# Two edge sorts of a graph kernel: records turned to column order by ScalarE, places summed on TensorE, loads and features reordered

## The chip, the cores and the metric

The kernel runs on one core of one Trainium2 chip. The metric is the device time of one execution in microseconds (us). The core has five engines with instruction streams of their own: TensorE (PE, matrix products, with weight loads, PEld, beside them), VectorE (DVE), ScalarE (ACT), GpSimd (POOL) and SyncE (SP, which here only issues transfers). Transfers (DMA) can be issued by SP, ACT and POOL, each a queue of its own.

## The reference

It has four residual stages on x of 3,125 nodes by 256 features. Source, destination, edge type and edge weight of 53,125 edges are given.

```
x = x + L0_gnn(layernorm(x), (src, dst), edge_weight)      # 4 heads of 64
x = x + L0_ffn(layernorm(x))                               # 16 experts, top 2
x = x + L1_gnn(layernorm(x), rel_emb, src, dst, edge_type) # 200 relations
x = x + L1_ffn(layernorm(x))                               # top half of the tokens

# L0_gnn
feats = einsum('nd,hdo->hno', x, Ws) + bs[:, None, :]
a_s = einsum('hno,ho->hn', feats, aw[:, :O]); a_d = einsum('hno,ho->hn', feats, aw[:, O:2*O])
score = a_s[:, src] + a_d[:, dst] + aw[:, 2*O][:, None] * elem[None, :] + ab[:, None]
w = exp(-relu(score / 20.0))
out = segment_sum(w * feats[:, dst], src) / segment_sum(w, src)
# L0_ffn: per expert, hidden = silu(x @ w1) * (x @ w2); out = hidden @ w3, weighted
# L1_gnn: agg = segment_sum((h[src] + rel_emb[etype]) @ weight_neighbor * alpha, dst)
#         alpha = exp(leaky_relu(score))[:, None], divided by its sum over that axis of one
#         out = relu(agg) + h @ (loop weights)
```

Both graph stages sum over the edges of each node. So the kernel needs the edges grouped by node: sort s0 by `src` for the first graph stage, sort s1 by `dst` for the second.

## The kernel before, in words

The nodes form NT = 25 blocks of 128. The edges lie in a table of 128 partitions by EC = 416 columns, seen as NS = 13 slices of SC = 32 columns; a group is SJ = 8 columns. An edge becomes a record of V fields of f16: 5 in s0 (other node, place in its block, three pieces of the weight's bits), 3 in s1. `sort_edges` makes the generator `ranking` (`load_in`, then `places`), 13 steps `move` and a function `load`.

`load_in` loads segment, other end and value (`load_edges`) and cuts them into digits `dig`. `bf` holds each edge's block number.

`places` computes where each edge goes. First it counts: for each block a one-hot comparison over the 416 columns (`hot`, L377, on DVE and POOL in turn in s0), then on PE for each of the 32 columns of a slice a matmul with all-ones weights and one with strictly-before weights over the 25 x 13 = 325 values of that column (L383; they stand 32 elements apart). From the counts come the start of each block and slice (`base`, L422). Then a loop over 25 blocks (L431 to L445) makes `x`, 1 where the edge is of block b, adds `base` to the first column of each slice, makes a running sum (`cum`, L437), keeps it where the edge is of block b (`own`, L441), and adds that into `pos` (L444, on POOL in s0). 13 rounds of three operations `ge` (L487, L493, L498) find the target rows `to` of the records' chunks; from `pos` come `pp` and `kp`, partition and place in a chunk.

`move(s)` handles a slice of 32 columns, in 4 groups of 8. A group makes on DVE the one-hots `hp` (L545, 128 x 8) and `hk` (L550, 40 x 8) and their product with the digits, `hv` (L555, NK x V x 8 elements: 1,600 in s0, 960 in s1; the 8 columns lie innermost). Then 8 matmuls per group (L560), with `hp[:, :, j]` as weights and `hv[:, :, :, j]` moving, accumulate in PSUM. After 4 groups ACT copies the sum out (`rec`, L566) and 5 indirect transfers on POOL scatter the chunks into the DRAM table `tab` (L569). `load` reads the table (`tk`, L588, on SP), turns it on PE (L601), and makes index, row and value of 440 edge tiles.

The order is that of the instruction streams that a scheduler makes from the program order; each engine then runs its own stream in order. `run` builds constants, zeroes the two edge tables (`edge_table`, SP transfers from a zero tile), makes the sort's constants, runs the s0 ranking, loads x, moves s0, zeroes the sums `sums0` and `sums1` of the two graph stages (`zero_sums`, L298: a POOL memset and SP transfers each), and then calls `heads_features` (weights `w_feat` and bias `b_feat` loaded on SP, extended by the products with `aw` at L858 and L861; for each of 25 blocks of normalised x two transposes L173, two matmuls L873, a bias addition on DVE L877; the table `table0` written by SP) and `load`. `heads_edges` gathers feature rows by indirect transfers (L754) and sums edges on PE (L798), with the s1 ranking as fill between its groups. `experts` runs 65 expert tiles (token rows gathered L1119, turned L173, products L1130 and L1147, Silu L1135) and calls one s1 `move` step in each of the first 13 tiles. Relation stage and token stage follow.

## Time and profile before

| what | value |
| --- | --- |
| runs | 2841.39, 2849.33 (median), 2865.01 us |
| the profiled execution | 2845.15 us, span 2842.8 us, mean granted clock 0.822 |
| PE busy | 1878.6 us, 66% |
| DVE busy | 1446.3 us, 51% |
| POOL busy | 1167.4 us, 41% |
| ACT busy | 390.7 us, 14% |
| first matmul of the s0 moves | at 170.1 us |
| first edge gather of the heads' stage | at 429.71 us |
| gathers of edge rows, L754 | 880, 848.6 us busy on POOL |
| s1 and s0 moves on PE, L560 | 832, 246.8 us busy |

Times inside the span count from the first instruction. The engine's busy time says how long it worked, not whether anything waited for it. A line such as `L560 PE MATMUL s_mv<-s_hv,s_hp 128*128 128x200 f16 x416 | 150.5, 543 | 89.9 <-DVE s_hv L555 89.9` names source line, engine, operation, output and inputs, shape and number of instructions; then the busy time in us and the mean of one in ns (overlapping matmuls make that mean longer than their distance); then the engine's idle time before them and what ended it. PEclk is the granted clock of PE as a share of full speed.

### The profile page before, as it was taken

What the parts mean: (1) busy time and instruction counts of PE and PEld (TensorE: products, weight loads), DVE (VectorE), ACT (ScalarE), POOL (GpSimd) and SP (SyncE); (2) the same over time, 40 slices, a digit from 0 to 9 for tenths busy, and PEclk for the clock granted to TensorE, in tenths of its full rate; (3) what the DMA queues carried; (4) which work ended last, traced back from release to release, by engine and by line L of the source; (5) the groups of instructions that cost most, each with busy time, mean ns of one, the idle gap of its engine ahead of it and who ended that gap; (6) DMA issues with size and microseconds to landing.
All of it is one profiled execution on the core that took longest, in us unless ns stands there. A gap on an engine that the chain in (4) does not pass through costs nothing.

```text
span 2842.8 us, 24381 instructions
## 1 busy us (share of the span) xinstructions
PE 1878.6 (66%) x7534; PEld 1126.4 (40%) x7534; DVE 1446.3 (51%) x3397; ACT 390.7 (14%) x1097; POOL 1167.4 (41%) x1198
## 2 busy tenths in 40 slices
PE   3169554854544443399999991447878778785298
PEld 0024232543433332356666660323434334343166
DVE  4876225476665343644422224445655556549721
ACT  0000010010000000100112120112222222221012
POOL 4235306576654646034411115036666666650000
PEclk9999996676666667577799996768889888898599
DMA  2000325343444433144499982254545455431000
GB/s 83 0 3 5 104 89 137 93 130 112 115 100 114 116 100 101 49 150 130 131 316 318 317 291 84 87 156 131 148 129 148 130 142 149 128 85 34 8 21 18
DMA packets 258938, 334.04 MB, mean 118 GB/s; under 512 B 30861, under 2 KB 192407, under 8 KB 258807
## 3 DMA queue, kind: packets, MB, share of 16 engines
q1 hardware_dynamic: 197527, 191.26, 21.3%
q0 software_dynamic: 51920, 132.68, 17.6%
q10 hardware_dynamic: 9360, 8.52, 0.9%
q8 instruction: 61, 1.00, 0.1%
q14 instruction: 70, 0.57, 0.1%
HBM read 298.38 MB, written 33.98 MB: 117 GB/s over the span
## 4 chain that ended last, share of the span: by engine, by line
PE 39%; DVE 14%; issue 10%; POOL 9%; another core or an unknown queue 8%; DMA 4%; ACT 1%; SPq 0%; DVEq 0%; POOLq 0%; ACTq 0%
PE ps_sums L798 10%; PE ps_h L1130 9%; POOL rows L754 9%; PE ps_y L1147 4%; PE s_mv L560 3%; DVE cmp L1426 3%; PE ps_hid L1453 3%; PE ps_out L1464 3%; DMA rows<-table,s_idx 3%; DVE msg L926 2%; DVE hot L771 2%; PE ps_x_t L173 1%; PE ps_h_t L173 1%; PE ps_f L1264 1%
## 5 line engine op out<-in xcount | busy, mean ns | idle before, releaser
L754 POOL DMA_INDIRECT rows<-table,s_idx x880 | 848.6, 964 | 725.0 <-issue 240.4
L798 PE MATMUL ps_sums<-msg,oh 128*128 128x260 f32 x880 | 306.6, 519 | 261.8 <-DVE msg L926 143.1
L798 PE MATMUL ps_sums<-rows,ohw 128*128 128x457 f32 x880 | 414.0, 616 | 62.8 <-ACT ohw L1319 54.1
L798 PEld LDWEIGHTS ps_sums<-msg,oh 128*128 128x128 f32 x880 | 226.6, 265 | 325.1 <-issue 250.1
L560 PE MATMUL s_mv<-s_hv,s_hp 128*128 128x200 f16 (+1 forms) x832 | 246.8, 472 | 89.9 <-DVE s_hv L555 89.9
L798 PEld LDWEIGHTS ps_sums<-rows,ohw 128*128 128x128 f32 x880 | 179.0, 215 | 217.5 <-issue 149.6
L1130 PE MATMUL ps_h<-w,x_t 128*128 128x512 f32 x520 | 256.1, 638 | 0.0
L771 DVE TENSOR_SCALAR hot<-wide,pcols 128x768 bf16<-128x768 bf16 (+1 forms) x296 | 175.4, 597 | 73.9 <-PE ps_near L780 63.0
L560 PEld LDWEIGHTS <-s_hp 128*128 128x128 f16 x832 | 122.1, 147 | 208.7 <-issue 180.3
L762 DVE TENSOR_TENSOR oh<-ps_hold,s_row 128x768 f32<-128x768 f32 (+1 forms) x148 | 139.9, 946 | 125.7 <-remote 73.5
L1119 POOL DMA_INDIRECT xg<-xtab,who x65 | 61.9, 952 | 345.1 <-PE ps_x_t L173 302.6
L569 POOL DMA_INDIRECT s_tab<-s_rec,s_to x130 | 147.8, 1137 | 115.1 <-ACT s_rec L566 78.9
L780 PEld LDWEIGHTS <-hot 128*128 128x128 bf16 x1760 | 70.0, 98 | 212.3 <-issue 149.2
L1136 DVE TENSOR_TENSOR hid<-hid,ps_h 128x512 f32<-128x512 f32 x65 | 44.7, 688 | 210.3 <-ACT hid L1135 204.4
L1319 ACT ACTIVATE ohw<-oh,s 128x128 f32<-128x128 f32 x440 | 136.5, 388 | 106.6 <-DVE s L1282 75.2
L1130 PEld LDWEIGHTS ps_h<-w,x_t 128*128 128x128 f32 x520 | 102.8, 209 | 105.7 <-issue 105.5
L926 DVE TENSOR_TENSOR msg<-rows,ps_hold 128x1536 f32<-128x1536 f32 x74 | 128.1, 1731 | 2.0 <-ACT ps_hold L924 1.9
L787 DVE TENSOR_REDUCE near<-ps_near 128x24 f32<-128x72 f32 (+2 forms) x148 | 29.4, 198 | 190.3 <-remote 150.2
L1147 PE MATMUL ps_y<-w,h_t 128*128 128x256 f32 x520 | 122.9, 379 | 0.7 <-ACT h_t L175 0.7
L1147 PEld LDWEIGHTS ps_y<-w,h_t 128*128 128x128 f32 x520 | 98.7, 190 | 41.7 <-issue 30.6
L545 DVE TENSOR_TENSOR s_hp<-num_p,s_pp 128x1024 f16<-128x1024 f16 x104 | 71.8, 690 | 82.8 <-PE s_mv L560 81.4
L1313 DVE TENSOR_TENSOR rows<-ps_hold,s_val 128x1200 f32<-128x1200 f32 x74 | 101.1, 1367 | 6.1 <-PE ps_sums L798 6.1
(307 smaller groups left out, 2344.2 us busy)
## 6 DMA issues: line engine op xcount, KB each, us to landing
w<-in_L_ffn_w_dram SPq DMA_DIRECT2D x195, 512.0 KB
wide<-s_w SPq DMA_DIRECT2D x72, 576.0 KB
rows<-table,s_idx POOLq DMA_INDIRECT x880
ytab<-y ACTq DMA_DIRECT2D x65, 128.0 KB
sums<-sums_z SPq DMA_DIRECT2D x5, 1142.5 KB
more<-sums SPq DMA_DIRECT2D x25, 228.5 KB
sums<-sums_z SPq DMA_DIRECT2D x5, 650.0 KB
table<-f SPq DMA_DIRECT2D x5, 650.0 KB
```

The lines of the kernel that those rows point to most:

```text
L560: nc.tensor.matmul(ps[:, : NK * V], hp[:, :, j], rec[:, :, :, j].rearrange("p k v -> p (k v)"), start=(j0 + j == 0), stop=(j0 + j == C - 1),)
L569: d = nc.gpsimd.indirect_dma_start(out=tab, out_offset=bass.IndirectOffsetOnAxis(ap=to[:, i : i + 1], axis=0), in_=out[:, k * CH * V : (k ...
L754: nc.gpsimd.indirect_dma_start(out=rows[:, j, :width], out_offset=None, in_=table, in_offset=bass.IndirectOffsetOnAxis(ap=st["idx"][:, k + ...
L762: nc.vector.tensor_tensor(oh[:, :n, :], numbers[:, None, :P].to_broadcast(sh), st["row"][:, k : k + n, None].to_broadcast(sh), op=OP.is_equal,
L771: nc.vector.tensor_scalar(t[:, : n // 2, :], w, at, None, op0=OP.is_equal)
L798: nc.tensor.matmul(ps[:, :W], oh[:, j, :], msg[:, j, :], start=(head and j == 0), stop=(last and j == n - 1),)
L926: nc.vector.tensor_tensor(msg[:, :n, :HO].rearrange("p j (h o) -> p j h o", o=O), rows[:, :n, :HO].rearrange("p j (h o) -> p j h o", o=O), ...
L1130: nc.tensor.matmul(ph[:, i * HID : (i + 1) * HID], xt[:, c, :], w12[:, i, c, :], start=(c == 0), stop=(c == C - 1),)
L1147: nc.tensor.matmul(py[:, :D], ht[:, c, :], w3[:, c, :], start=(c == 0), stop=(c == HC - 1))
L1313: nc.vector.tensor_tensor(rows[:, :n, R0:], self.numbers[:, None, :R].to_broadcast(sh), st["val"][:, k : k + n, None].to_broadcast(sh), op ...
L1319: nc.scalar.activation(ow[:, j, :], oh[:, j, :], AF.Copy, scale=s[:, 1, j : j + 1])
L1426: nc.vector.tensor_scalar(cmp[:, s:e], wrow[:, s:e], w, None, op0=op, op1=OP.add, accum_out=rank[:, t, i : i + 1],)
```

## The change

The change has six parts.

1. Loads: `load_edges` fills only the partitions from 96 on with padding, on DVE. The s0 edges are loaded first, then x; the zeroing of the edge tables moves out of `edge_table` into `zero_table`, called after the loads (s0) and after the features' weights (s1).
2. Counts of s0 (`roomy`): block numbers as bf16 with columns outermost (`bt`), compared with a table of block numbers (`num_b`) in 4 DVE operations of 2,600 elements; `hot` has columns outermost, so that the 64 matmuls read 325 elements in one piece.
3. Places of s0: ACT copies `x` from `hot`; PE sums `pos` in PSUM by 26 matmuls with the identity; the operations `ge` take up to 7 slices at once.
4. Moves of both sorts: ACT copies the group's records `hv` (in `rec`) into `col`, where the records of one column lie in one piece, and the matmuls read `col`. The s1 moves are cut into halves: 26 steps in 26 expert tiles.
5. `load` of s0 issues its reads from POOL's queue.
6. `heads_features` is split: `heads_weights` before the moves, the features after moves and `load`. The bias is added by a third matmul (`top`, a matrix whose first row is ones, times `bias`), ACT copies the result out, and ACT's queue writes `table0`. The sums are zeroed last in program order.

```diff
@@ -224,7 +224,7 @@
-        engine.memset(dst, pad)
+        engine.memset(dst[96:, :], pad)
         done = 0
@@ -286,6 +286,11 @@
+        return tab
+    def zero_table(self, name, tab):
+        nc, CH, n = self.nc, self.CH, self.MT + self.OT
+        V = tab.shape[1] // CH
         with self.tc.tile_pool(name=f"{name}_init", bufs=1) as pool:
@@ -293,7 +298,6 @@
-        return tab
@@ -329,15 +333,15 @@
-            return rp.tile([P, EC], dt, tag="row", name=f"{name}_{nm}", bufs=16 if roomy else 7)
+            return rp.tile([P, EC], dt, tag="row", name=f"{name}_{nm}", bufs=8 if roomy else 7)
...
-            self.load_edges(seg_i, seg, self.NP, help)
+            self.load_edges(seg_i, seg, self.NP, nc.vector)
             oth_i = tmp(I32, "oth")
-            self.load_edges(oth_i, other, 0, help)
+            self.load_edges(oth_i, other, 0, nc.vector)
             val = tmp(F32 if bits else I32, "val")
-            self.load_edges(val, value, 0, help)
+            self.load_edges(val, value, 0, nc.vector)
             yield
@@ -345,6 +349,9 @@
+            if roomy:
+                st["bt"] = tl([P, C, NS], BF16, "bt")
+                nc.vector.tensor_copy(st["bt"], bi.rearrange("p (s t) -> p t s", t=C))
@@ -368,8 +375,27 @@
-            piece = NT if roomy else -(-NT // 2)
-            for b0 in range(0, NT, piece):
+            if roomy:
+                num_b = tl([P, n], BF16, "num_b").rearrange("p (b s) -> p b s", s=NS)
+                nc.vector.tensor_copy(
+                    num_b, self.iota[:, :NT, None].to_broadcast([P, NT, NS])
+                )
+                hot = tl([P, C, n], BF16, "hot")
+                for t0 in range(0, C, J):
+                    sh = [P, J, NT, NS]
+                    nc.vector.tensor_tensor(
+                        hot[:, t0 : t0 + J, :].rearrange("p t (b s) -> p t b s", s=NS),
+                        num_b[:, None].to_broadcast(sh),
+                        st["bt"][:, t0 : t0 + J, None, :].to_broadcast(sh), op=OP.is_equal,
+                    )
+                    for w, ps in ((self.ones_h, tot), (self.before_h, pre)):
+                        for t in range(t0, t0 + J):
+                            nc.tensor.matmul(
+                                ps[:, :n], w, hot[:, t, :], start=(t == 0), stop=(t == C - 1)
+                            )
+            piece = -(-NT // 2)
+            for b0 in () if roomy else range(0, NT, piece):
                 m = min(piece, NT - b0)
@@ -426,23 +452,37 @@
-            pos = tl([P, EC], F32, "pos")
-            nc.vector.tensor_scalar(pos, bf, float(NT), 8191.0, op0=OP.is_ge, op1=OP.mult)
-            for b in range(NT):
-                x = tmp(F32, "x")
-                nc.vector.tensor_scalar(x, bf, float(b), None, op0=OP.is_equal)
+            def run(b, own, x):
                 xs = x.rearrange("p (s t) -> p s t", t=C)[:, :, 0]
...
-                own = tmp(F32, "own")
                 nc.vector.scalar_tensor_tensor(
...
-                help.tensor_tensor(pos, pos, own, op=OP.add)
-                yield
+            if roomy:
+                pos = self.ps_b(f"{name}_pos")[:, :EC]
+                own = tmp(F32, "own")
+                nc.vector.tensor_scalar(own, bf, float(NT), 8192.0, op0=OP.is_ge, op1=OP.mult)
+                nc.tensor.matmul(pos, self.ident, own, start=True, stop=False)
+                hv = hot.rearrange("p t (b s) -> p b s t", s=NS)
+                for b in range(NT):
+                    x, own = tmp(F32, "x"), tmp(F32, "own")
+                    nc.scalar.copy(x.rearrange("p (s t) -> p s t", t=C), hv[:, b])
+                    run(b, own, x)
+                    nc.tensor.matmul(pos, self.ident, own, start=False, stop=(b == NT - 1))
+            else:
+                pos = tl([P, EC], F32, "pos")
+                nc.vector.tensor_scalar(pos, bf, float(NT), 8192.0, op0=OP.is_ge, op1=OP.mult)
+                for b in range(NT):
+                    x, own = tmp(F32, "x"), tmp(F32, "own")
+                    nc.vector.tensor_scalar(x, bf, float(b), None, op0=OP.is_equal)
+                    run(b, own, x)
+                    help.tensor_tensor(pos, pos, own, op=OP.add)
+                    yield
@@ -482,21 +522,23 @@
-            for s in range(NS):
-                ge = tl([P, KC, 2 * NT], F32, "ge", bufs=2)
+            few = 7 if roomy else 1
+            for s0 in range(0, NS, few):
+                m = min(few, NS - s0)
+                ge = tl([P, few, KC, 2 * NT], F32, "ge", bufs=1 if roomy else 2)[:, :m]
+                sh = [P, m, KC, 2 * NT]
+                def of_block(v):
+                    return v[:, s0 : s0 + m].rearrange("p s i b -> p s (i b)")[
+                        :, :, None, :
+                    ].to_broadcast(sh)
                 nc.vector.tensor_tensor(
-                    ge, qv[:, s, :, None].to_broadcast([P, KC, 2 * NT]),
-                    edge[:, s].rearrange("p i b -> p (i b)")[:, None, :].to_broadcast(
-                        [P, KC, 2 * NT]
-                    ), op=OP.is_ge,
-                )
-                nc.vector.tensor_tensor(
-                    ge, ge, jump[:, s].rearrange("p i b -> p (i b)")[:, None, :].to_broadcast(
-                        [P, KC, 2 * NT]
-                    ), op=OP.mult,
-                )
-                nc.vector.tensor_reduce(at[:, s, :], ge, AX.X, OP.add)
-                if s % 3 == 2:
+                    ge, qv[:, s0 : s0 + m, :, None].to_broadcast(sh), of_block(edge), op=OP.is_ge
+                )
+                nc.vector.tensor_tensor(ge, ge, of_block(jump), op=OP.mult)
+                nc.vector.tensor_reduce(at[:, s0 : s0 + m, :], ge, AX.X, OP.add)
+                if s0 % 3 == 2:
                     yield
@@ -536,10 +578,12 @@
-        def move(s, mp):
+        def move(s, mp, cols=range(0, C, J)):
             pp, kp, dig, to = st["pp"], st["kp"], st["dig"], st["to"]
-            ps = self.ps_b(f"{name}_mv")
-            for j0 in range(0, C, J):
+            if cols[0] == 0:
+                st["ps"] = self.ps_b(f"{name}_mv")
+            ps = st["ps"]
+            for j0 in cols:
                 t0 = s * C + j0
@@ -556,12 +600,16 @@
+                col = tl([P, J, NK * V], F16, "col", mp, bufs=3)
+                nc.scalar.copy(col, rec.rearrange("p k v j -> p j (k v)"))
                 for j in range(J):
...
-                        ps[:, : NK * V], hp[:, :, j],
-                        rec[:, :, :, j].rearrange("p k v -> p (k v)"),
+                        ps[:, : NK * V], hp[:, :, j], col[:, j, :],
                         start=(j0 + j == 0), stop=(j0 + j == C - 1),
...
+            if cols[-1] + J < C:
+                return
             out = tl([P, NK * V], F16, "rec", mp, bufs=3)
@@ -585,7 +633,9 @@
-                    ld = nc.sync.dma_start(tk[:m, i], rows[i * m : (i + 1) * m])
+                    queue = nc.gpsimd if roomy else nc.sync
+                    ld = queue.dma_start(tk[:m, i], rows[i * m : (i + 1) * m])
                     for s in sent:
@@ -632,7 +682,12 @@
-        return ranking(), [lambda mp, s=s: move(s, mp) for s in range(NS)], load
+        if roomy:
+            return ranking(), [lambda mp, s=s: move(s, mp) for s in range(NS)], load
+        halves = [range(0, C // 2, J), range(C // 2, C, J)]
+        return ranking(), [
+            lambda mp, s=s, h=h: move(s, mp, h) for s in range(NS) for h in halves
+        ], load
@@ -825,7 +880,7 @@
-    def heads_features(self):
+    def heads_weights(self, pool):
@@ -842,7 +897,7 @@
-        with self.tc.tile_pool(name="feat", bufs=2) as pool:
+        if True:
@@ -861,6 +916,20 @@
+            self.top = pool.tile([P, P], F32, name="top_row", bufs=1)
+            nc.gpsimd.affine_select(
+                out=self.top, in_=self.ones, compare_op=OP.is_ge, fill=0.0, base=0,
+                pattern=[[0, P]], channel_multiplier=-1,
+            )
+            self.w_feat = w, bias
+    def heads_features(self, pool):
+        nc, NT, D, H = self.nc, self.NT, self.D, self.H
+        HO, C = H * self.O, D // P
+        w, bias = self.w_feat
+        if True:
             xn = self.layer_norm("xn0")
@@ -872,11 +941,12 @@
-                            start=(c == 0), stop=(c == C - 1),
+                            start=(c == 0), stop=False,
                         )
-                    nc.vector.tensor_add(f[:, t - t0, :], pf[:, : HO + 2 * H], bias)
+                    nc.tensor.matmul(pf[:, : HO + 2 * H], self.top, bias, start=False, stop=True)
+                    nc.scalar.copy(f[:, t - t0, :], pf[:, : HO + 2 * H])
                 nc.vector.tensor_copy(self.near0[:, t0 : t0 + n, :], f[:, :n, HO + H :])
-                nc.sync.dma_start(t0v[:, t0 : t0 + n, :], f[:, :n, : self.W0])
+                nc.scalar.dma_start(t0v[:, t0 : t0 + n, :], f[:, :n, : self.W0])
@@ -1482,24 +1552,30 @@
-        with tc.tile_pool(name="sort_c", bufs=1) as consts:
-            self.sort_constants(consts)
+        with tc.tile_pool(name="sort_c", bufs=1) as consts, ExitStack() as ctx0:
             with tc.tile_pool(name="sort0", bufs=1) as pool:
-                with tc.tile_pool(name="rank0", bufs=1) as rank:
-                    ranking, steps, load = self.sort_edges(
-                        pool, rank, "s0", a["src"], a["dst"], a["edge_weight"], True, tab0,
-                        nc.gpsimd, True,
-                    )
-                    for _ in ranking:
-                        pass
+                rank = ctx0.enter_context(tc.tile_pool(name="rank0", bufs=1))
+                moves = ctx0.enter_context(tc.tile_pool(name="move0", bufs=1))
+                feat = ctx0.enter_context(tc.tile_pool(name="feat", bufs=2))
+                ranking, steps, load = self.sort_edges(
+                    pool, rank, "s0", a["src"], a["dst"], a["edge_weight"], True, tab0,
+                    nc.gpsimd, True,
+                )
+                next(ranking)
                 self.load_x()
-                with tc.tile_pool(name="move0", bufs=1) as moves:
-                    for step in steps:
-                        step(moves)
+                self.zero_table("s0", tab0)
+                self.sort_constants(consts)
+                for _ in ranking:
+                    pass
+                self.heads_weights(feat)
+                self.zero_table("s1", tab1)
+                for step in steps:
+                    step(moves)
+                st = load()
+                self.heads_features(feat)
+                ctx0.close()
                 self.sums0 = self.zero_sums("sums0", self.D + a["L0_gnn_Ws"].shape[0])
...
-            self.heads_features()
-            st = load()
             with tc.tile_pool(name="sort1", bufs=1) as pool:
...
```

## The prediction

> **What bounds the kernel now.** I read the 40 slices first (71 us each; PE's busy share in tenths).
>
> ```profile
> PE   3169554854544443399999991447878778785298
> ```
>
> The first six digits cover the first edge sort and the features: little PE work, so something serial. The table of windows (columns: PE, PEld, DVE, ACT, POOL busy, granted clock, DMA share, GB/s) says what.
>
> ```profile
> 50.00:100.00 50.00, 30.18 (x56) 6.70 (x54) 26.38 (x63) 0.00 (x0) 5.81 (x5) 1.00 0.00 0
> 100.00:150.00 50.00, 0.00 (x0) 0.00 (x0) 50.00 (x108) 0.00 (x0) 15.71 (x16) 1.00 0.01 0
> 200.00:250.00 50.00, 50.00 (x140) 20.32 (x139) 32.05 (x53) 1.30 (x4) 25.30 (x21) 1.00 0.03 5
> 300.00:350.00 50.00, 20.84 (x59) 8.49 (x57) 10.15 (x16) 1.02 (x3) 18.49 (x16) 1.00 0.33 107
> 1240.00:1255.00 15.00, 15.00 (x57) 9.62 (x55) 7.43 (x15) 1.44 (x3) 6.14 (x7) 0.77 0.40 132
> 1500.00:1506.00 6.00, 6.00 (x24) 3.70 (x23) 1.54 (x3) 1.18 (x2) 0.94 (x1) 1.00 0.97 327
> ```
>
> From 50 to 100 the counting on PE runs, from 100 to 150 DVE alone (50.00 of 50), from 200 to 250 PE alone, from 300 to 350 nothing is full. ACT is nearly empty. In the experts the clock is 0.77 with the second sort's moves between the tiles (1240) and 1.00 without (1500). PE is full in both. The groups by shape of the first 450 us give prices.
>
> ```profile
> L560 PE MATMUL s_mv<-s_hv,s_hp 128*128 128x200 f16 x416 | 150.5, 543 | 89.9 <-DVE s_hv L555 89.9
> L383 PE MATMUL s_tot<-s_hot,ones_h 128*128 128x325 bf16 x32 | 17.6, 722 | 45.1 <-POOL s_hot L377 45.1
> L555 DVE TENSOR_TENSOR s_hv<-s_hk,s_dig 128x1600 f16<-128x1600 f16 x52 | 51.3, 986 | 0.0
> L437 DVE TENSOR_TENSOR_SCAN s_cum<-at_block,s_x 128x416 f32<-128x416 f32 x25 | 25.4, 1014 | 0.2
> L435 DVE TENSOR_TENSOR s_x<-s_x,s_base 128x13 f32<-128x13 f32 x25 | 16.1, 643 | 0.1
> L441 DVE SCALAR_TENSOR_TENSOR s_own<-s_bf,s_cum 128x416 f32<-128x416 f32 x25 | 14.6, 582 | 0.2
> L469 DVE TENSOR_TENSOR s_edge<-room,s_gend 128x325 f32<-128x325 f32 x1 | 0.7, 720 | 0.0
> L175 ACT COPY x_t<-ps_x_t 128x256 f32<-128x256 f32 x25 | 9.3, 372 | 87.8 <-PE ps_x_t L173 87.8
> ```
>
> 416 matmuls of 200 columns lie end to end from 170.1 to 320.9, so 150.8/416 = 0.363 us each or 1.67 ns per column (plus 0.03); 64 of 325 columns take 45.1 to 80.1, 0.545 each, the same 1.67 ns. Both read operands with gaps (16 and 64 bytes). PE's f32 passes on contiguous data take 3.44 us for 8 of 512 columns (an expert tile at 1500), 0.84 ns per column; an f32 matmul is recorded as two passes. L435 handles 13 elements but takes 0.643 on average: in the trace it takes 0.17 when POOL is idle and 0.92, ending with POOL's L444, when not. L469 reads 325 values 52 bytes apart in 0.720, a contiguous 325-element operation takes 0.32 to 0.49. ACT copies 256 contiguous elements in 0.372 and 512 in 0.587: 0.157 + 0.84 ns per element.
>
> The timeline of the sort's end (start, duration, what ended the idle time):
>
> ```profile
> 344.02 6.84 SPq L307 DMA_DIRECT2D sums<-sums_z  x5
> ...
> 365.67 0.43 DVE L858 TENSOR_TENSOR w_tmp<-w_feat,aw 128x256 f32<-128x256 f32 x1 [50.98 <-DMA w_feat<-in_L_gnn_Ws_dram]
> ...
> 420.28 1.52 SPq L588 DMA_DIRECT2D s_tk<-s_tab  x4
> ...
> 429.71 1.29 POOL L754 DMA_INDIRECT rows<-table,s_idx  x1 [85.71 <-DVE near0p L651]
> ```
>
> The last scatters end near 327.5. Then SP zeroes two sums tables from 328.9 on, and the weights `w_feat`, queued behind them, arrive at 365.67. DVE stood still 51 us. Features take 365.7 to 416.8, the table write lands, the records are turned, and the first gather goes at 429.71. All before it is one serial stretch. In the experts' timeline:
>
> ```profile
> 1342.29 5.46 PE L560 MATMUL s_mv<-s_hv,s_hp 128*128 128x120 f16 x24
> ...
> 1350.55 4.38 PE L1130 MATMUL ps_h<-w,x_t 128*128 128x512 f32 x8
> ...
> 1504.23 3.60 PE L1130 MATMUL ps_h<-w,x_t 128*128 128x512 f32 x8
> ```
>
> 32 of the second sort's matmuls (24 and 8, 0.2208 to 0.24 each, 7.06 per tile) stand between the matmuls of an expert tile. Tiles with such a fill have a pitch of 14.77, of which 7.74 is the tile's own, and tiles without it 5.82. Thirteen tiles have it.
>
> **The change, part by part.** All durations are from one profiled execution; the sum starts from its 2845.15 us (span 2842.8), 4.2 under the runs' median.
>
> *Loads first.* The s0 edges go to SP ahead of x, and the whole-tile memset on POOL becomes a 32-row one on DVE. Before, the loads went at 12.5, the one-hots at 19.9. The first x block, issued at 0.8, was used at 5.7, so edges should be in at 6 to 7, and the one-hots start at about 12.5: gain 7.4. x waits behind them; the features need it late. The s0 table's zeroing follows x on SP, long before the scatters.
>
> *Counts.* 25 one-hot operations and 64 gapped matmuls become 4 DVE comparisons of 2,600 elements and 64 contiguous matmuls. No row has such a comparison. At the rate of L555 (0.986 for 1,600 f16) it is 1.5 us, at that of L762 (0.946 for 768 f32, 1.23 ns per element) 2.9 to 3.2. I take 2.1. A 325-column matmul lies between 0.06 (L780, 12 columns) and 0.27 (the f32 rate). 4 x 2.1 plus the last batches and the conversions of `bt` and `num_b`: 15.5 us instead of 60.4, bounds 10.5 to 21.5. Gain 45 (39 to 50).
>
> *Places.* DVE loses `x` (0.28 pitch) and, with POOL's additions gone, the stall in L435; the scan (0.94 pitch) and `own` (0.50) stay: 25 x (0.10 + 0.94 + 0.50) = 39, with a start of 2. What was elsewhere is now queued in DVE's stretch: 6 weight products with reductions (4.5), 25 normalisations (8.5), statistics (3.2). The comparisons `ge` shrink from 13 x 1.2 = 15.5 to 10.5, as the fixed 0.145 of each falls away. The 325-element operations, casts and conversions stay, 13.5. Sum 82 against 85.2 measured (80.2 to 165.4). ACT's 25 gapped copies of 416 (0.5 at its contiguous rate, 0.85 at 1.67 ns) and PE's 26 identity matmuls (two f32 passes of 416 x 0.84 ns = 0.70) hide under DVE's 39; if ACT's were over 1.54 us, ACT would set the loop. Gain 3, bounds 0 to 15.
>
> *Moves of s0.* From the end of ranking to the first matmul 4.6 us as before. ACT copies each group's 1,600 records into `col`, reading f16 values 16 bytes apart. No row has ACT reading like this. Bounds: the contiguous 0.157 + 1,600 x 0.84 = 1.50 below, and above, with 1.67 ns (PE) and 1.77 to 2.03 (DVE's L469, and L1065 with 400 strided elements in 0.961) 2.8 to 3.4. I choose 2.75 pitch, from PE's rate over the very same operand and gap. ACT is then the bound: 52 x 2.75 + 13 x 0.25 (rec copies) = 146.3 against 150.8. DVE (0.60 + 0.23 + 0.91 = 1.74 per group, 90.5) and PE (416 contiguous, 23 to 83) lie under it. Gain 4.5 only.
>
> *Between moves and gather.* The sums are zeroed beside the moves (in the changed order POOL's first memset stands ahead of the scatters, the second behind five of them), so the stall of 38 us from 327.5 to 365.7 goes. Were this cover gone, SP's 20 us of zeroing would delay the second sort's loads only. After the last matmul: record copy and issue 1.8, five scatters 6.3 (5 x 1.26), landing 2.5, four issues of the `tk` load on POOL's queue about 5, landing 2.7, turning 1.5: 20. POOL is idle then, so the moved load delays only itself. In PE's order 20 turns stand ahead of the 25 feature tiles and wait for that load and so overlap with nothing. A feature tile has 6 instead of 4 passes: its pitch was 1.895 (4 x 0.25 + 0.47 + 0.43), and with a third matmul for the bias 2.44 (1.7 if everything on PE runs at 0.84 ns per column, 2.5 at its rate here): 25 x 2.44 = 61 instead of 51. ACT takes the evacuation and five issues of 0.34, between copies of 0.37, under PE's pitch. Landing and first gather 5.6, as the write took 4.1 in a quieter stretch. Sum 86.6 against 108.8 from 320.9 to 429.7: gain 22 (0 to 40).
>
> First gather: 12.5 + 15.5 + 82 + 4.6 + 146.3 + 86.6 = 347.5, gain 82.
>
> *Heads.* Tiles and their gathers are untouched; up to 7 us could come from 13 one-hots that now stand ahead. I take 0.
>
> *Experts.* The moves of s1 come in halves over 26 tiles, 16 contiguous matmuls of 120 columns each: 0.055 (L780) to 0.22 (as now), taken 0.11 (0.84 ns per column). Tile: 5.82 + 1.76 = 7.58, over 26: 197. Before: 13 x 14.77 + 13 x 5.82 = 268. Gain 71 (93 at 0.055). ACT has per tile two copies of 960 (1.65 each at 1.67 ns) and 1.65 of its own: 4.95, hidden under 7.58. DVE's two groups of 1.5 and POOL's 2.5 scatters fit as well. This needs the clock of 1.00.
>
> Sum: 2845.2 - 82 - 71 = **2692 us**.
>
> **Rivals.**
> R1, ScalarE (ACT) reads with gaps as fast as without: DVE bounds the moves, 52 x 1.74 + 4 = 94.5 instead of 146.3, so 2640. For: ACT's rows are all at 0.84 ns and PSUM-fed, no gap has been tried. Against: PE and DVE both pay twice for a gap. The Trainium skill, "ScalarE: Activation LUTs", section "What ACT_TABLE_LOAD costs", gives 186 ns plus 0.833 ns per element and names no layout: an estimated 1.52 us per copy, R1's case. "Advanced Engine Details and Errata" of the Trainium skill, section "SBUF Cachelines", says the other: a different 16-byte line with each access is penalised. No run here shows ScalarE doing either.
> R2, the clock does not rise: PE stays dense, the granted clock stays 0.77 in the filled tiles. Tile 7.74 + 16 x 0.15 = 10.15, gain 4 instead of 71: 2759. For: the clock falls with the fill now (0.77 against 1.00). Against: PE is full in both windows, and the fill's PE time falls by three quarters.
> R3, slower: the gapped copy on ACT takes the place of PE as bound. With X us per copy of 1,600, the moves take 52X + 3.3 and an expert tile 1.2X + 1.65 once that exceeds 7.58. All gains are eaten at X = 5.4 (3.3 ns per element). At 4 ns, X = 6.56: moves 344, first gather 546 (116 lost), tiles 9.5 (71 - 51 = 20 won): 2941. For: this engine is now alone on the path, unpriced. Against: the worst gapped row is 2.03 ns.
> R4, the change does not do what it says: the weights (`hp`, 16-byte gap, unchanged) and not the moving records set PE's pitch. Moves then 151, fill 16 x 0.2208, tile 9.35, gain 25: 2743. Against: L383 has contiguous weights and the same 1.67 ns.
>
> **How the numbers follow.** Forecast 0.53, R1 0.23, R2 0.12, R4 0.04, R3 0.08 (0.02 of it near break-even). The range takes in R1 with the lower bound of the counts (2640 - 5) and the cheapest fill (-23), 2612, and R2 with the counts at their upper end (+6), 2765; little beyond R3 is left out. About 1%, 28 us, can be told from no change: faster 0.53 + 0.23 + 0.12 + 0.04 = 0.92, same 0.02, slower 0.06.
>
> **What would show it.** Right: the first gather near 347; `col` copies on ACT at 2.7 to 2.9 with ACT nearly full from 115 to 261; PE matmuls of 200 columns at half their time or less; no idle of 51 us ahead of the weight products; feature tiles at 2.4; expert tiles near 7.6 for 26 tiles with a clock near 1.00. R1: `col` at 1.5 and DVE full in the moves. R2: tiles of 10 at a clock below 0.8. R3: `col` above 5. R4: matmuls of 200 columns still at 0.36. The prediction is wrong if the gather comes after 400, or if the heads' stage, which I price at nothing, grows.

## The result and the profile after

The changed kernel takes 2673.69 us (median, 2669.22 to 2684.40) beside 2845.55 for the kernel before: a ratio of 0.939, 95% interval 0.934 to 0.944. It is 171.9 us faster; 153 were forecast. The profiled execution took 2670.88 us with a span of 2669.1.

The 40 slices of the changed kernel, PE's busy share (67 us each):

```profile
PE   3644647645544453399999904377887878764498
```

The stretch ahead of the first edge gather fills some five slices now (352 us) instead of six (430 us of 71 each). Where the time went is read from the same marks in both traces:

| stretch | before, us | forecast | after, us |
| --- | --- | --- | --- |
| start to the one-hots | 19.8 | 12.5 | 12.7 |
| one-hots and counts, to the last matmul of the counts | 60.4 | 15.5 | 12.2 |
| places and ranking, to the end of the place sums | 85.2 | 82 | 81.1 |
| to the first matmul of the moves | 4.7 | 4.6 | 8.0 |
| moves of the first sort | 150.7 | 146.3 | 157.2 |
| to the first edge gather | 108.9 | 86.6 | 80.9 |
| first edge gather at | 429.7 | 347.5 | 352.1 |
| first edge gather to first expert gather | 783.7 | 783.7 | 775.5 |
| first to last expert gather | 465.8 | 395 | 375.4 |
| last expert gather to the end | 1163.6 | 1163.6 | 1166.1 |

So 77.6 us come from the start, 8.2 from the heads' stage, 90.4 from the experts, and 2.5 are lost behind them. The windows of the changed kernel (PE, PEld, DVE, ACT, POOL busy, granted clock, DMA share, GB/s) show what bounds each stretch now:

```profile
50.00:115.00 65.00, 39.63 (x51) 12.19 (x52) 62.02 (x140) 24.32 (x24) 1.18 (x1) 0.53 0.07 21
115.00:200.00 85.00, 41.41 (x224) 35.56 (x223) 50.29 (x83) 85.00 (x36) 38.15 (x32) 0.50 0.32 100
1160.00:1200.00 40.00, 39.97 (x216) 26.85 (x215) 25.68 (x52) 28.59 (x27) 22.92 (x21) 1.00 0.90 275
```

Places: DVE is busy 62 of 65 us. Moves: ACT 85.00 of 85, where PE was the full one before. Experts: PE full at a granted clock of 1.00, with the second sort's moves in it. The groups by shape for the first 420 us give the new prices (the mean of overlapping matmuls is longer than their distance):

```profile
L605 ACT COPY s_col<-s_hv 128x1600 f16<-128x1600 f16 x52 | 157.4, 3115 | 3.2 <-DVE s_hv L599 3.2
L607 PE MATMUL s_mv<-s_col,s_hp 128*128 128x200 f16 x416 | 77.5, 366 | 87.6 <-ACT s_col L605 86.0 <-DVE s_bf L350 1.5
L599 DVE TENSOR_TENSOR s_hv<-s_hk,s_dig 128x1600 f16<-128x1600 f16 x52 | 51.0, 983 | 0.3 <-ACT s_col L605 0.3
L387 DVE TENSOR_TENSOR s_hot<-s_num_b,s_bt 128x2600 bf16<-128x2600 bf16 x4 | 6.3, 1605 | 0.0
L394 PE MATMUL s_tot<-s_hot,ones_h 128*128 128x325 bf16 x32 | 6.2, 345 | 14.3 <-DVE s_hot L387 14.3
L476 PE MATMUL s_pos<-s_own,ident 128*128 128x416 f32 x50 | 43.9, 981 | 36.5 <-DVE s_own L462 36.2
L474 ACT CAST s_x<-s_hot 128x416 f32<-128x416 bf16 x25 | 23.7, 965 | 54.1 <-DVE s_own L462 49.1 <-DVE s_hot L387 3.7 <-DVE s_x L457 1.3
L457 DVE TENSOR_TENSOR s_x<-s_x,s_base 128x13 f32<-128x13 f32 x25 | 4.3, 171 | 0.2 <-ACT s_x L474 0.2
```

A `col` copy of 1,600 takes 3.1 us (2.75 forecast, 1.5 for a contiguous read). VectorE's `hv` kept its 0.98, so ScalarE alone is new on that path. The gapped copy of 416 (L474) takes 0.965, where 0.85 was the upper estimate, still under DVE's work per block. The comparison for the counts takes 1.6, and in the timeline eight of L394's matmuls start 1.13 after the eight before them, 0.14 each instead of 0.545. The 13-element L457 fell from 0.643 to 0.171. PE's place sums (L476) are a new cost beside DVE, not ahead of it: the two passes of one block take 1.75, just under the 1.84 that a block takes on DVE at the end of the loop. The timeline of POOL at the end of the sort, and that of an expert tile:

```profile
279.87 2.51 POOL L638 DMA_DIRECT2D s_tk<-s_tab  x4 [1.44 <-DMA s_tab<-s_rec,s_to]
352.06 1.11 POOL L809 DMA_INDIRECT rows<-table,s_idx  x1 [69.68 <-DVE near0p L706]
```

```profile
1165.31 1.13 PE L607 MATMUL s_mv<-s_col,s_hp 128*128 128x120 f16 x16
...
1166.43 1.93 ACT L605 COPY s_col<-s_hv 128x960 f16<-128x960 f16 x1 [1.94 <-PE ps_y L1217]
...
1166.95 3.60 PE L1200 MATMUL ps_h<-w,x_t 128*128 128x512 f32 x8
```

The read of the sorted records is issued at 279.9, 9 us after the last move; the features follow it, and the gather goes at 352.1 (the idle 69.68 is POOL's, which has nothing else to do). In the expert tile 16 matmuls now take 1.13 us, 0.0706 each, instead of 0.22.

### The profile page after: what moved, and what is told of

Same layout as the page of the kernel before. It is cut to its first block, busy times and chain, and to the rows that moved or that the text cites. A ratio compares the mean times of both kernels' runs of the same rounds, so it can differ in the third digit from the quotient of the medians.

```text
span 2669.1 us, 24633 instructions
## 1 busy us (share of the span) xinstructions
PE 1745.7 (65%) x7636; PEld 1103.2 (41%) x7636; DVE 1408.5 (53%) x3314; ACT 668.2 (25%) x1251; POOL 1124.8 (42%) x1159
## 5 line engine op out<-in xcount | busy, mean ns | idle before, releaser
L853 PE MATMUL ps_sums<-msg,oh 128*128 128x260 f32 x880 | 300.4, 509 | 231.4 <-DVE msg L996 90.7
L605 ACT COPY s_col<-s_hv 128x1600 f16<-128x1600 f16 (+1 forms) x104 | 257.8, 2524 | 50.1 <-PE s_mv L607 25.0
L1200 PE MATMUL ps_h<-w,x_t 128*128 128x512 f32 x520 | 236.5, 598 | 0.0
L607 PE MATMUL s_mv<-s_col,s_hp 128*128 128x200 f16 (+1 forms) x832 | 107.5, 295 | 87.6 <-ACT s_col L605 86.0
L994 ACT ACTIVATE ps_hold<-s 128x24 f32<-128x24 f32 x74 | 14.3, 194 | 568.1 <-DVE s L991 125.4
L607 PEld LDWEIGHTS <-s_hp 128*128 128x128 f16 x832 | 96.7, 156 | 102.3 <-issue 96.1
L1200 PEld LDWEIGHTS ps_h<-w,x_t 128*128 128x128 f32 x520 | 94.6, 192 | 94.2 <-issue 93.9
```

The costliest lines, as they stand in the source:

```text
L605: nc.scalar.copy(col, rec.rearrange("p k v j -> p j (k v)"))
L607: nc.tensor.matmul(ps[:, : NK * V], hp[:, :, j], col[:, j, :], start=(j0 + j == 0), stop=(j0 + j == C - 1),)
L853: nc.tensor.matmul(ps[:, :W], oh[:, j, :], msg[:, j, :], start=(head and j == 0), stop=(last and j == n - 1),)
L1200: nc.tensor.matmul(ph[:, i * HID : (i + 1) * HID], xt[:, c, :], w12[:, i, c, :], start=(c == 0), stop=(c == C - 1),)
```

## The experiments

The kernels ran on several chips. On two of them the kernel before takes 2636 to 2647 us, on the others 2837 to 2847. In the changed kernel's two traces the heads' stage differs by 137 us between the two kinds of chip, and the stretch from the last expert gather to the end by 59; the stretch up to the first edge gather and the experts agree. So each run is compared by what it saves against the kernel before on its own chip, and by the marks of its trace. The changed kernel saves 171.9 us on the first chip, and, run again beside two of the experiments, 172.2.

**The changed kernel again.** No edit.

> The changed kernel itself, beside the others on one chip: first gather at 352, expert tiles of 6.8, and the ratio to before near 0.939 as measured; a ratio under 0.93 or over 0.95 would say that the ratio depends on the chip.

Measured 2475.18 beside 2647.40, ratio 0.935 (0.932 to 0.937), first edge gather at 352.2, first to last expert gather 373.9, filled expert tiles of 6.8. The saving is the same in microseconds; the ratio depends on the chip a little, within the bounds that were set.

**The first sort without the copy.**

```diff
-                col = tl([P, J, NK * V], F16, "col", mp, bufs=3)
-                nc.scalar.copy(col, rec.rearrange("p k v j -> p j (k v)"))
+                if not roomy:
+                    col = ...; nc.scalar.copy(col, ...)
...
-                        ps[:, : NK * V], hp[:, :, j], col[:, j, :],
+                        ps[:, : NK * V], hp[:, :, j],
+                        col[:, j, :] if not roomy else rec[:, :, :, j] (k v)
```

> The changed kernel, but the first sort's matmuls read the records with gaps again, without ScalarE's copy; the second sort keeps the copy. Theory (each stage lasts as long as its fullest engine): in the changed kernel ScalarE's 52 copies of 3.0 us set the first sort's moves, 157 us and 3 us of waiting for the first copy. Without them PE is the bound at 0.363 per matmul, 151 us, and the first matmul comes 3 us earlier: first gather at about 342 instead of 352, time about 2664, some 10 us less than the changed kernel. Rival (reading in one piece pays here too): gapped matmuls cost more than 0.363 in the new surroundings, the moves take 170 us or more and the time is 2690 or more.

Ratio 0.932 (0.930 to 0.934), 181.7 us saved, 9.5 more than the changed kernel; first matmul at 109.9, moves 150, first gather at 341.4. The theory holds within about a microsecond in all these marks: in the first sort the copy is a loss. Its window from 115 to 250:

```profile
115.00:250.00 135.00, 135.00 (x376) 54.81 (x375) 84.73 (x139) 3.91 (x12) 69.50 (x57) 0.50 0.22 63
```

PE is full again (135 of 135), at the same 0.36 us per gapped matmul as in the kernel before, although the record shows a granted clock of 0.50 here and 1.00 there.

**The second sort without the copy**, halves kept (the same edit with `roomy`).

> The changed kernel, but the second sort's matmuls read with gaps, without the copy; the halves over 26 expert tiles stay. Theory (the reading in one piece is what makes the filled expert tile short): 16 matmuls of 0.22 instead of 0.07, the tile 9.3 instead of 6.9, over 26 tiles 62 us more at a full clock, 90 to 115 more where the clock falls to 0.77 again: time 2735 to 2785. Rival (spreading over 26 tiles is what pays): time within 15 us of the changed kernel's 2674, tiles about 7.

Ratio 0.968 (0.966 to 0.970), 83.9 us saved, 88 fewer. That is between the theory's two cases. First to last expert gather is 461.7, against 465.8 before the change, so the halves alone are worth some 4 us, on traces of two chips. A pair of filled tiles takes 20.3 us, 10.15 each. The window inside:

```profile
1100.00:1200.00 100.00, 100.00 (x367) 63.78 (x366) 43.98 (x88) 12.74 (x25) 34.05 (x35) 0.90 0.58 182
```

PE is full, clock 0.90. With the copies the clock is 1.00. So the reading in one piece carries the experts' gain, in two ways: 26 x 16 matmuls are 0.15 us shorter (62 us), and the tile's own matmuls run at the full clock: the eight products `ps_h` of a tile take 3.6 us there (0.450 each) and 4.2 here (0.522 each).

**The second sort in whole slices**, copies kept.

```diff
-        halves = [range(0, C // 2, J), range(C // 2, C, J)]
+        halves = [range(0, C, J)]
```

> The changed kernel, but the second sort moves a whole slice per expert tile again, in 13 tiles, with the copies. Theory: ScalarE then has four copies of 1.93 and 1.7 of its own per tile, 9.4, more than PE's 5.8 + 32 x 0.07 = 8.0, so 13 x 9.4 + 13 x 5.8 = 198 us instead of 178, time up by about 20, 2694. Rival (the copies are hidden however they are spread): PE sets 13 x 8.0 + 13 x 5.8 = 179, time unchanged within 5. Second rival (a denser fill lowers the clock): tiles of 10.6 and more, time up by 35.

Ratio 0.948 (0.946 to 0.950), 137.6 us saved, 34.6 fewer; first to last expert gather 408.1 us, 34 more than in the changed kernel's run, the filled tile 10.4. The direction is the theory's, the size is the second rival's, and both have a share: the clock is 0.91 to 0.97, and PE, unlike in the case without copies, is not full. It waits for ScalarE (start, duration, what ended the wait):

```profile
1061.57 0.96 PE L607 MATMUL s_mv<-s_col,s_hp 128*128 128x120 f16 x8 [1.83 <-ACT s_col L605]
...
1072.20 0.65 PE L607 MATMUL s_mv<-s_col,s_hp 128*128 128x120 f16 x8 [1.17 <-ACT s_col L605]
```

From 1020 to 1140 PE is busy 101.75 of 120 us, so in a tile of some 10.6 us it works 9.0 and waits 1.6, mostly for a copy that it needs in the middle of the tile. The 9.0 are themselves 1.2 more than twice the changed kernel's fill would give (5.8 + 2 x 1.0), so the work that goes with the lower clock adds nearly as much as the waits do; whether one brings on the other is not shown. ScalarE is not full either (87.83 of 120). So halves pay only together with the copies: some 4 us without them, 34 with them.

**The old order at the end of the first sort.** Sums zeroed after the moves in a pool of their own, then the features' weights loaded, features, then the records read. The buffers of ranking and moves are given back earlier too.

```diff
-                self.heads_weights(feat)
...
-                st = load()
-                self.heads_features(feat)
-                ctx0.close()
                 self.sums0 = self.zero_sums(...)
                 self.sums1 = self.zero_sums(...)
+            with tc.tile_pool(name="feat", bufs=2) as feat:
+                self.heads_weights(feat)
+                self.heads_features(feat)
+            st = load()
```

> The changed kernel with the old order at the end of the first sort: both sums zeroed after the moves, then the features' weights loaded, the features, and last the reading of the sorted records; counts, places, copies, bias matmul and queues as changed. Theory: the stall of 38 us ahead of the weight products comes back and the features overlap a little with the reading of the records again (10 less): first gather 25 to 35 later than 352, time about 2702. Rival (the zeroing would be hidden in any order, the tail's gain comes from elsewhere): time within 8 of 2674.

Ratio 0.953 (0.951 to 0.955), 123.3 saved, 48.9 fewer. The first gather comes at 391.6, 39.5 later than 352.1, above the 25 to 35 expected. The rest, 9 us, lies behind it (the heads' stage is 5.7 longer; in the other versions on chips of this kind it takes from 632 to 642). The stall is back:

```profile
281.82 20.46 SPq L311 DMA_DIRECT2D sums<-sums_z  x10
...
316.90 0.42 DVE L913 TENSOR_TENSOR w_tmp<-w_feat,aw 128x256 f32<-128x256 f32 x1 [52.06 <-DMA w_feat<-in_L_gnn_Ws_dram]
```

Ten zeroing transfers stand on SP ahead of the weights, and DVE waits 52 us. That the records are read while nothing else waits was expected to give back 10 us and gave nothing: the read is issued at 382.5, once the feature table has landed, so it does not overlap the features in this order either. The places end at 101.9 here instead of 106.0: the weight products are no longer in DVE's stretch.

**The bias on VectorE.**

```diff
-                            start=(c == 0), stop=False,
+                            start=(c == 0), stop=(c == C - 1),
...
-                    nc.tensor.matmul(pf[...], self.top, bias, start=False, stop=True)
-                    nc.scalar.copy(f[:, t - t0, :], pf[...])
+                    nc.vector.tensor_add(f[:, t - t0, :], pf[...], bias)
```

> The changed kernel, but the bias is added by VectorE while it takes the features out of PSUM, as before, instead of a third matmul and a ScalarE copy; the late place of the features stays. Theory: PE sets the features, two passes of the bias matmul are 0.45 of the 2.35 per tile, so 25 x 0.45 = 11 us less: first gather at 341 instead of 352. Rival (the chain of transposes, ScalarE's copy and matmuls sets a tile, the bias matmul lies beside it): first gather within 3 us of 352.

Ratio 0.936 (0.931 to 0.941), 183.6 saved, 11.7 more; too near for the interval alone, but the first gather is at 340.0 instead of 352.1. The theory holds: the third matmul costs its two passes, and the old evacuation by VectorE was free here.

**The places summed by POOL.**

```diff
-                pos = self.ps_b(f"{name}_pos")[:, :EC]
+                pos = tl([P, EC], F32, "pos")
...
-                    nc.tensor.matmul(pos, self.ident, own, start=False, stop=(b == NT - 1))
+                    help.tensor_tensor(pos, pos, own, op=OP.add)
```

> The changed kernel, but the places are summed by POOL in SBUF instead of by PE with the identity (and one row buffer fewer); ScalarE still copies x. Theory: while POOL adds, VectorE's 13-element addition takes 0.92 instead of 0.17; that was 0.47 per block on average before, so 25 x 0.47 = 12 us more in the place loop: end of the places at about 118 instead of 106, first gather 10 to 12 later. Rival (PE's identity products, 1.8 us each at the low clock in the trace, are as long as VectorE's 1.85 per block and hold it back): end of the places within 4 of 106 or earlier.

Ratio 0.945 (0.940 to 0.950), 154.6 saved, 17.3 fewer; the places end at 121.7 instead of 106.0, first gather 368.1. The theory holds and a little more: L457's mean is back at 0.681, and 25 x 0.51 are 13 of the 16 us.

```profile
L457 DVE TENSOR_TENSOR s_x<-s_x,s_base 128x13 f32<-128x13 f32 x25 | 17.0, 681 | 0.0
```

**Three groups in five copied.** In the first sort only.

```diff
-                col = tl(...)
-                nc.scalar.copy(col, ...)
+                if not roomy or (t0 // J) % 5 % 2 == 0:
+                    col = tl(...); nc.scalar.copy(col, ...)   # the others read rec with gaps
```

> The changed kernel, but in the first sort only three groups in five are copied by ScalarE; for the others PE reads the records with gaps. Theory: ScalarE then has 31 x 3.0 + 4 = 97 us, PE 31 x 1.49 + 21 x 2.9 = 107, VectorE 91, so the moves take about 107 to 112 instead of 157 and the first gather comes at about 305, 47 earlier. Rival (the engines wait for each other in turn, since each has its groups in order): moves of 130 or more, gain under 25.

Ratio 0.935 (0.930 to 0.941), 184.9 saved; moves 148 us, first gather at 343.5. The rival holds. No engine is full:

```profile
120.00:250.00 130.00, 91.22 (x359) 55.61 (x358) 80.38 (x133) 85.79 (x39) 64.58 (x56) 0.50 0.19 54
```

The timeline names the ring: DVE's `hp` waits for PE to leave an older group, ScalarE waits for the `hv` behind that `hp`, PE for the copy.

```profile
164.81 6.06 ACT L606 COPY s_col<-s_hv 128x1600 f16<-128x1600 f16 x2 [3.29 <-DVE s_hv L599]
165.96 0.69 DVE L589 TENSOR_TENSOR s_hp<-num_p,s_pp 128x1024 f16<-128x1024 f16 x1 [1.01 <-PE s_mv L608]
...
167.92 1.49 PE L608 MATMUL s_mv<-s_col,s_hp 128*128 128x200 f16 x8 [1.99 <-ACT s_col L606]
```

**The same with deeper buffers.**

```diff
-                hp = tl([P, P, J], F16, "hp", mp, bufs=3)
+                hp = tl([P, P, J], F16, "hp", mp, bufs=5 if roomy else 3)
...
-                rec = tl([P, NK, V, J], F16, "hv", mp, bufs=3)
+                rec = tl([P, NK, V, J], F16, "hv", mp, bufs=4 if roomy else 3)
```

> The mix of three copied groups in five, with five buffers instead of three for the one-hots hp, four instead of three for the records, and, for room, two row buffers fewer and three slices at a time in ge (some 2 us more in the places). In the mix with three buffers the moves took 148 us with no engine full. Theory (each group's hp waits until PE has left the group three before, so the engines run in step): with deeper buffers the moves take 110 to 120 and the first gather comes at about 315. Rival (ScalarE's queue, in which each slice's record copy waits for PE ahead of the next slice's copies, keeps the step): moves of 140 or more, first gather 340 or later.

Ratio 0.927 (0.925 to 0.929), 196.4 saved; moves 134, first gather at 327.7. It lies between the two: 14 us of the step went. A wait of the kind that the rival named remains: ScalarE's copy of a slice's result waits for PE, 35.5 us over the twelve copies of this view, with the next groups' copies queued behind it. Whether that wait sets the 134 us is not shown; no run takes it alone out of this mix.

```profile
L617 ACT CAST s_rec<-s_mv 128x200 f16<-128x200 f32 x12 | 3.9, 328 | 35.5 <-PE s_mv L608 35.5
```

**The copy with the gap on the other side**, both sorts: read in one piece, written with gaps.

```diff
-                nc.scalar.copy(col, rec.rearrange("p k v j -> p j (k v)"))
+                nc.scalar.copy(col.rearrange("p j n -> p n j"), rec.rearrange("p k v j -> p (k v) j"))
```

> The changed kernel, but ScalarE's copy runs in the other order in both sorts: it reads the records in one piece and writes them with gaps of 400 bytes (240 in the second sort) instead of reading with gaps of 16 bytes and writing in one piece. Theory (the gap in what is read makes the price): a copy of 1,600 takes about 1.5 us instead of 3.0, VectorE's 1.74 per group becomes the bound of the first sort's moves, 95 us instead of 157, first gather at about 290 instead of 352. Rival (a gap costs the same on either side): copies of 2.7 us or more, first gather within 12 of 352.

Ratio 1.058 (1.056 to 1.060), 153.8 us slower than the kernel before. Both expectations fell: a copy of 1,600 takes 7.4 us, first gather at 556.6.

```profile
L605 ACT COPY s_col<-s_hv 128x1600 f16<-128x1600 f16 x45 | 314.6, 7382 | 3.2 <-DVE s_hv L599 3.2
```

This is rival R3 of the prediction with X = 7.38: by its formula the moves take 387, a filled tile 10.5, and some 164 us are lost; 154 were. The total is near partly by luck: the moves took 358, as the copies start only 7.0 apart, and a filled tile 11.3.

**The features among the moves.** Five of six groups copied, bias and the turned x taken by VectorE, table written by SP.

```diff
-                for step in steps:
+                rows = self.heads_features(feat)   # yields after five tiles
+                for i, step in enumerate(steps):
                     step(moves)
+                    if i % 2:
+                        next(rows, None)
                 st = load()
-                self.heads_features(feat)
```

> Built from the parts: the changed kernel with five of six groups copied by ScalarE, the bias added and the turned x copied by VectorE, and the 25 feature tiles placed among the moves of the first sort, five after every second slice, the table written by SP. Theory: moves and features together last as long as PE needs, 43 x 1.49 + 9 x 2.9 + 25 x 1.9 = 138, with ScalarE at 134 and VectorE at 112, instead of 157 + 59 one after the other; first gather at about 270 to 280, 72 to 82 earlier than 352. Rival (in bunches of five the tiles hold up the copies and the copies the tiles): moves and features 175 or more, gain under 40.

Ratio 0.920 (0.915 to 0.924), 231.6 us saved, 60 more than the changed kernel. First gather at 294.8: 57 earlier, between theory and rival. Moves and features together take 163 us (112.8 to 275.7) instead of 138, and none of PE, ACT and DVE is full:

```profile
112.00:276.00 164.00, 117.34 (x566) 86.27 (x565) 113.96 (x232) 134.81 (x57) 74.12 (x61) 0.72 0.26 80
```

**The same with deeper buffers and the slice's copy two groups later.**

```diff
+                if roomy and j0 == J and st.get("tail"):
+                    st.pop("tail")()        # record copy and scatters of the slice before
```

> The version with the features among the moves, now with five buffers for hp, four for the records, and each slice's record copy on ScalarE issued two groups into the next slice, so that it no longer waits for PE ahead of further copies (for room two row buffers fewer and ge by three slices, some 2 us more in the places). Theory (lock step was what held moves and features at 150 us with PE 111, ScalarE 125 and VectorE 104 busy): they now take 137 to 142, first gather at 284 to 290 instead of 295. Rival (ScalarE's 44 copies of 3.1 and PE's bunches of features stay in turn): first gather at 295 to 300, no gain over that version.

Ratio 0.920 (0.917 to 0.924), 224.1 saved, first gather at 292.1: 2.7 earlier than the version before, well short of the theory, and no gain in time that can be measured. Moves and features take 160 us, with ScalarE busy 134 of 160 (the 150 in the expectation leaves out the last slice). The later place of the slice's copy did only part of what it was meant to do: ScalarE still waits 11.3 us for PE ahead of these copies, after 15.4 in the version before. Which wait holds moves and features stays open. Both versions are faster than the kernel before and the changed kernel; the one with the features among the moves is the simpler.

## Why the prediction was right

The saving came out 19 us larger than forecast. That is the size of the miss in the experts alone; the other errors cancel. They do so up to the first gather, too: counts, places and the tail of the sort came out 10 us better than forecast, first matmul and moves 14 us worse. So 352.1 for a forecast of 347.5 is closer than the single terms were.

**Loads, counts, places.** Each right within 3.5 us. The comparison of 2,600 elements took 1.60 (2.1 taken, 1.5 the lower bound). The run with POOL's additions shows that the stall in the 13-element addition was POOL's. The stretch of the places gained 4 and not these 16, because other work of DVE stands in it now. In the last blocks, where DVE has nothing else, a block takes 1.8 us instead of 2.9; in the blocks with one normalisation each it takes 2.5. The weight products moved in as well (4 us, by the old order's run), and so did the chain from the counts to `edge` (some 6 us, estimated from its rows), which ran beside PE's counting before. The forecast's terms for this stretch, as written, add up to some 81 and not 82. PE's passes for one block took 1.75 at a granted clock of 0.53, where 0.70 was taken; they stay hidden, but barely.

**First matmul.** The step "4.6 us as before" failed: 8.0. It left out that the first copy (3.1) stands between the first records and the first matmul.

**Moves of the first sort.** The mechanism was right, ScalarE is the bound; its price was 3.0 in distance instead of 2.75, so a small gain of 4.5 became a loss of 6.4. With the step above the copy costs the first sort 9.5 to 10.7 us, and the run without it shows just that. R1 fell with it: by the two copy sizes an element costs (3.12 - 1.93)/640, 1.85 ns, against 0.84 without gaps. The Trainium skill's figure ("ScalarE: Activation LUTs", section "What ACT_TABLE_LOAD costs") fits the contiguous rows (0.372 for 256, an estimated 0.40) and not this copy, which took 3.1 where it gives an estimated 1.52. The Trainium skill's "Advanced Engine Details and Errata", section "SBUF Cachelines", which says that a different line with each access is penalised, agrees with the trace in direction. The prediction called all of ACT's rows fed from PSUM; L527 in its own trace is not (416 elements from SBUF, without gaps, in 0.538), so reading SBUF as such is not what makes the copy dear.

**Between moves and gather.** 80.9 for 86.6. The stall of 38 us was the zeroing ahead of the weights: with the old order it is back and the gather 39.5 later. What the change pays for it is the bias matmul, 12 us, shown by its removal. The tile took 2.35 (2.44 forecast); the features began 15 us after the last matmul instead of 20.

**Heads.** Forecast at nothing, 8.2 us came, 1 above the bound of 7. No run isolates it, and it may be nothing: in the versions measured on chips of the same kind this stage takes from 769 to 789 us, where the edits do not touch it. So these 8 us are no success of the prediction and no miss that can be explained.

**Experts.** The largest miss in size: 90.4 for 71. The term "0.11 per matmul" was too high. The filled tile takes 6.80, so each of its 16 added matmuls costs (6.80 - 5.82)/16 = 0.061, and 26 x 16 x 0.049 = 20 us are the whole miss. That the tile's own part returns to 5.8 at a full clock was right, and R2 with it wrong. The windows from the first to the last expert gather show it, before and after (the granted clock is the third figure from the end):

```profile
1213.00:1679.00 466.00, 462.14 (x1711) 290.39 (x1712) 162.47 (x324) 72.75 (x131) 129.66 (x129) 0.89 0.72 234
1128.00:1503.00 375.00, 371.81 (x1712) 241.34 (x1713) 160.21 (x317) 159.40 (x180) 133.85 (x130) 0.99 0.92 290
```

R4 fell: with the unchanged gapped weights a matmul of 120 columns takes 0.07.

**R3** did not occur in the change, but its break-even was a real one: the same copy with the gap on the writing side lies beyond it.

## What to carry to other kernels

An engine that rearranges data for another one helps only where it has slack in that very stage: the same copy gains 88 us in the experts, where ScalarE was idle beside PE, and loses about 10 in the first sort, where it became the bound. Before moving work, sum each engine's time in that stage and look at which one is full afterwards. Where no engine is full, look for the ring of buffers: deeper ones gave 14 us in one version here, and hardly any in another, where the wait was not found. And look at what stands ahead of a small load on its queue: with ten zeroing transfers between the moves and the weights the first gather came 40 us later.

## What was not expected of the hardware

- ScalarE copying f16: 1.85 ns per element when it reads with gaps of 16 bytes and writes in one piece, 4.7 ns when it reads in one piece and writes with gaps of 400 bytes, (7.38 - 4.37)/640, and 0.84 in f32 rows from PSUM without gaps. No row has ScalarE reading f16 without gaps.
- A gapped f16 matmul of 200 columns takes the same 0.36 us whether the record shows a granted clock of 1.00 (before) or 0.50 (first sort without the copy). A contiguous one took 0.186 for 200 columns (1.49 for 8) at 0.50, and 0.071 for 120 columns (1.13 for 16) at 1.00.
- The changed kernel's heads' stage took 775 us on one chip and 638 on another, and the stretch behind the experts 1166 and 1107, while the stretch ahead of the heads and the experts agreed within 2 us. What differs in those stages was not tried.
